# Post-norm decoder layer on one core: turned softmax blocks laid out in runs of 2 KB, two buffers for them

## The chip, the cores and the metric

The kernel runs on one core of one Trainium2 chip. The metric is the device time in microseconds (us) of one execution of the whole program; three runs were taken. All arrays are float32 unless said otherwise. The engines are named as in the profile: PE (matrix multiplications), DVE (vector), ACT (scalar), POOL (GpSimd), and SP, which here only issues DMAs; "SPq" and "ACTq" are the DMA issues of SP and ACT.

## What is computed

Eight slices `t` of 512 rows by 512 columns pass through three blocks, each followed by a residual sum and a layer norm. Cut to what matters:

```python
# 1: relative-position attention among the 8 slices, for each of the 512 positions
x = layernorm(x + attn(x, pos, ...))
# 2: cross-attention, for each t, to a context of 512 rows x 1024
k, v  = split((ctx @ W_src.T + b_src) * mask)          # 8 heads of 64
q     = (x @ W_tgt.T + b_tgt) * mask
p     = softmax(where(mask == 0, -inf, q k / 8))        # [8 heads, 512 queries, 512 keys]
upd   = p @ v                                           # [512, 512]
x = layernorm(x + concat([x, upd]) @ W_out.T + b_out)
# 3: feed-forward
h = float8(relu(x @ w1.T + b1))                         # 2048 wide
x = layernorm(x + float16(h @ float8(w2).T + float16(b2)))
```

The change is in block 2. There `p` comes out of the scores with the queries on the partitions, and the product `p @ v` needs it with the keys on the partitions, so every 128x128 piece of `p` has to be transposed.

## The kernel before

**Two stages.** Stage A (up to about 930 us) does block 1 and, interleaved, the keys and values of block 2 for t = 0 to 6, which go to DRAM (`kd`, `vd`). Stage B (from L630) does blocks 2 and 3 for all t and is where the change lies.

**A unit of attention.** Stage B cuts block 2 into 64 units `u = (t, c, jj)`: `c` is one of four pairs of heads, `jj` one half of the queries (two tiles `j = 2 jj, 2 jj + 1` of 128 queries). `scores` (L740) runs one unit:

- PE: four score products `s` into PSUM (L751).
- DVE: minimum of the negated scores, for each of the two tiles and two heads (`exponentials`, L763); ACT: the exponential, with its sum (L773), into a buffer `pe` of the pool `sp` (7 buffers).
- DVE: division by the sum (`divide`, L788), then `turn_blocks` (L800): a transposition of 32x32 blocks in place of partition, from `pe` into a tile `pb`. Four such instructions fill one `pb`. The pool `pb` has one buffer.
- SP: `move_blocks` (L805): after the block transposition, each 32x32 block is turned but stands in the wrong group of 32 partitions. 16 DMAs, SBUF to SBUF, each from 32 partitions `32 g` to 32 partitions `32 a`, put them into `pT`. Each moves 64 KB. `pT` has one buffer, which two units (jj = 0 and 1) fill half by half.

`attend` (L836) then multiplies `pT` with the values (`av`, L845, eight matmuls, 16 records in the trace) and ACT copies the result to `uT` (L852). So, for one (t, c): the moves of its first unit can begin once the `av` of the pair before has read `pT`, and `av` can begin once the moves of its second unit have landed.

**The order of work.** The order on PE, DVE, ACT and SP is written out by the kernel itself, one instruction stream per engine, in program order. `weave` (L1096) lays the units of attention of slice t between the "dense" steps: the output projection of slice t-1 (`project_out`, L857), the transposition of the next slice's rows (`turn`, L720), the query projections (`queries`, L726), and the feed-forward of slice t-1 (`hidden_steps`, L933) and t-2 (`finish`, L1012). The DVE parts of a unit are put into a list `side` and drawn from it bit by bit (`run`, L673); `settle` (L659) draws until no item of a name is left. A finished unit's moves go to a list `moves` and are issued at the next `run` for which `pT` is free (`move`, L669).

**What else SP issues.** SP works through its own list in order: the loads of keys and values (L716, L718), the weights of the feed-forward (L922, or L926 to L931 in the first round, which also wait for sums on POOL), the mask (L699), the stores of the result (L1045), and the rows of the next slice (`load_x1`, L712), which reuse the buffer from which the result of slice t-2 is stored. `next_x1` (L1088) draws the normalizations and stores of t-2 and then issues that load.

Of the kernel before, what the change touches and what calls it, by code (L numbers as in the profile page):

```python
# [9 lines left out]
F32 = mybir.dt.float32  # L10
# [7 lines left out]
P = 128  # L18
# [6 lines left out]
S, FS, H2, D2 = 512, 1024, 8, 64  # L25
# [17 lines left out]
def decoder_layer(  # L43
# [586 lines left out]
    with ExitStack() as ph:  # L630

        def pool(name, bufs, **kw):
            return ph.enter_context(
                tc.tile_pool(name=name, bufs=bufs, reuse_waits="tile", **kw)
            )
# [2 lines left out]
        qx = pool("qx", 1)  # L638
        mp = pool("mp", 1)
        kvd = pool("kvd", 2)  # L640
        sp = pool("sp", 7)
        pbp = pool("pb", 1)
        ptp = pool("ptp", 1)
        sm = pool("smb", 4)
        ps_mm = pool("b_mm", 2, space=PSUM)
# [13 lines left out]
        def settle(tag):  # L659

            for q in (urgent, side):
                while any(item[0] == tag for item in q):
                    q.pop(0)[2]()
# [46 lines left out]
        def load_x1(t):  # L710
            x1[t] = qx.tile([P, NJ, E], F32, tag="x1", bufs=3, name=f"x1{t}")
            nc.sync.dma_start(x1[t], x1d[t].rearrange("j p e -> p j e"))  # L712
# [27 lines left out]
        def scores(t, c, jj):  # L740
            if c == 0 and jj == 0:
                uT[t] = qx.tile([P, EC, S], F32, tag="uT", name=f"uT{t}")
            prs, pss = [], []
            u = (t * EC + c) * 2 + jj
            settle(("e", u - 1))
            js = [2 * jj, 2 * jj + 1]
            for j in js:

                ps = ps_s.tile([P, 2, S], F32, tag="s", name=f"s{t}_{c}_{j}")
                for h in range(2):  # L750
                    nc.tensor.matmul(  # L751
                        ps[:, h, :],
                        lhsT=qT[t][half[h], c, j * P : (j + 1) * P],
                        rhs=kT[t, c][half[h], :],
                        start=True,
                        stop=True,
                    )
                pss.append(ps)

            def exponentials(i, h):  # L760
                j, ps, (nmax, den, _) = js[i], pss[i], small[i]
                pe = sp.tile([P, S], F32, tag="pe", name=f"pe{t}_{c}_{j}_{h}")
                nc.vector.tensor_tensor_reduce(  # L763
                    out=pe,
                    in0=ps[:, h, :],
                    in1=mb[t],
                    scale=1.0,
                    scalar=FMAX,
                    op0=ALU.add,
                    op1=ALU.min,  # L770
                    accum_out=nmax[:, h : h + 1],
                )
                nc.scalar.activation(  # L773
                    pe,
                    pe,
                    AF.Exp,
                    bias=nmax[:, h : h + 1],
                    scale=-1.0,
                    accum_out=den[:, h : h + 1],
                )  # L780
                prs.append(pe)

            def divide(i):
                _, den, rden = small[i]
                nc.vector.reciprocal(rden, den)
                for h in range(2):
                    pe = prs[2 * i + h]
                    nc.vector.tensor_scalar(  # L788
                        pe, pe, rden[:, h : h + 1], None, ALU.mult
                    )  # L790

            def turn_blocks(i):


                if i == 0:
                    prs.append(
                        pbp.tile([P, 2, ST, 4, 2, 32], F32, tag="pb", name=f"pb{u}")
                    )
                for h in range(2):
                    nc.vector.transpose(  # L800
                        prs[4][:, h, :, :, i, :].rearrange("p k a e -> p (k a) e"),
                        prs[2 * i + h].rearrange("p (c e) -> p c e", e=32),
                    )

            def move_blocks():  # L805

                if jj == 0:
                    pT[t, c] = ptp.tile([P, 2, ST, S], F32, tag="pT", name=f"pT{t}_{c}")
                for a in range(4):
                    for g in range(4):  # L810
                        q0 = g * P + jj * 64
                        nc.sync.dma_start(  # L812
                            pT[t, c][32 * a : 32 * a + 32, :, :, q0 : q0 + 64],
                            prs[4][32 * g : 32 * g + 32, :, :, a].rearrange(
                                "p h k j e -> p h k (j e)"
                            ),
                        )


            small = [  # L820
                [
                    sm.tile([P, 2], F32, tag=n, name=f"{n}{t}_{c}_{j}")
                    for n in ("nmax", "den", "rden")
                ]
                for j in js
            ]
            for i, h in ((0, 0), (0, 1), (1, 0)):
                side.append((("e", u), 1.0, lambda i=i, h=h: exponentials(i, h)))
            side.append((u, 1.2, lambda: divide(0)))
            side.append((("e", u), 1.0, lambda: exponentials(1, 1)))  # L830
            side.append((u, 1.2, lambda: turn_blocks(0)))
            side.append((u, 1.2, lambda: divide(1)))
            side.append((u, 1.2, lambda: turn_blocks(1)))
            side.append((u, 0.0, lambda: moves.append((u, move_blocks))))

        def attend(t, c):  # L836

            nonlocal attended
            settle((t * EC + c) * 2 + 1)
            move()  # L840
            attended += 1
            av = mm(f"av{t}_{c}")
            for s in range(ST):
                for h in range(2):
                    nc.tensor.matmul(  # L845
                        av[half[h], :],
                        lhsT=v[t, c][:, s, half[h]],
                        rhs=pT[t, c][:, h, s, :],
                        start=(s == 0),
                        stop=(s == ST - 1),  # L850
                    )
            nc.scalar.copy(  # L852
                uT[t][:, c, :].rearrange("p (j g e) -> p g j e", j=NJ, g=4),
                av.rearrange("p (g j e) -> p g j e", g=4, j=NJ),
            )
# [229 lines left out]
                nc.sync.dma_start(b2f, rows[R_B2].partition_broadcast(P))  # L1085
                side.append((("b2", 0), 0.5, lambda: nc.vector.tensor_copy(b2q, b2f)))

        def next_x1(t):  # L1088

            settle(("y", t - 2))  # L1090
            load_x1(t + 1)

        def of(cost, f, *a):
            return [(cost, False, lambda: f(*a))]

# [50 lines left out]
        with tc.manual_schedule(engines={ET.PE, ET.DVE, ET.Activation, ET.SP}):  # L1146
# [11 lines left out]
            for t in range(T):  # L1158
# [51 lines left out]
                else:  # L1210
# [12 lines left out]
                    if early:  # L1223
                        dense += done[early - 1]
                    dense += out4[0]
                    if 1 < t < T - 1:
                        dense += of(0.0, next_x1, t)
                    dense += out4[1] + out4[2] + turns[0] + turns[1] + out4[3]
                    projected = len(dense)
                    dense += turns[2] + turns[3] + asked[0]  # L1230
                    rest = asked[1:-1] if t + 1 < T else done[early:]
# [140 lines left out]
```

## Time and profile before

| | |
|---|---|
| median of three runs | 2444.47 us (2444.20 to 2444.59) |
| the profiled execution | 2444.88 us |
| its span, first to last instruction | 2443.1 us |
| stage A, 0 to 930 us | PE busy 880.45 us |
| t = 0, window 930 to 1090 us | PE busy 118.22 of 160 us |
| t = 1, window 1190 to 1352 us | PE busy 122.87 of 162 us |
| t = 7, window 2150 to 2330 us | PE busy 134.74 of 180 us |
| tail, 2330 to 2443 us | PE busy 103.58 us |
| all DMA queues | q1 (issued by SP) 263.33 MB, 42.4% of the 16 DMA engines' time |

A line of a group reads: source line, engine, operation, output <- inputs, shapes, number of instructions, then after the bar the busy time of all, the mean of one in ns, and the idle time of the engine just before them with what ended most of it. A line of a timeline reads: start in us, length in us, engine, line, operation, number of instructions merged, and in brackets the idle time of the engine before it and what ended it. A line of SP's timeline merges neighbouring issues of one line, waits between them included.

### The profile page before, as it was taken

The numbers are of one execution on the slowest core, as the hardware profiler recorded it, in microseconds if no ns is written. First come the engines' busy times: TensorE is split into PE (matmuls) and PEld (weight loads), VectorE is DVE, ScalarE is ACT, GpSimd is POOL, SyncE is SP. The second block draws the span as 40 slices with busy tenths as digits, with TensorE's granted clock in tenths as the row PEclk, the third lists the DMA queues.
The fourth block names the chain that finished last, engine by engine and source line by source line (L and its number), as shares of the span: only waits on it lengthen the run. The fifth ranks groups of instructions, "written<-read, shape, count | busy, mean of one in ns | idle before, by whom it ended". The sixth has DMA issues, their size and how long they took to land.

```text
span 2443.1 us, 22426 instructions
## 1 busy us (share of the span) xinstructions
PE 2129.4 (87%) x7552; PEld 1218.5 (50%) x7552; DVE 1520.0 (62%) x2542; ACT 591.8 (24%) x1325; POOL 167.6 (7%) x156
## 2 busy tenths in 40 slices
PE   8999999999899998765868889889889898996698
PEld 5654764664575673222434354453544544533456
DVE  4899999999999933343435545546555464554324
ACT  2011111101111112121322342342433333413212
POOL 1001100110010000021020001001000000000000
PEclk9999999999999999887988999999999999998899
DMA  8031630341242376545454565464554655744512
GB/s 300 31 108 35 215 125 18 128 170 43 95 164 95 117 256 198 108 87 112 93 138 110 108 162 112 99 156 101 118 132 89 164 118 103 161 73 108 119 40 94
DMA packets 395204, 293.38 MB, mean 120 GB/s; under 512 B 288977, under 2 KB 317649, under 8 KB 395089
## 3 DMA queue, kind: packets, MB, share of 16 engines
q1 hardware_dynamic: 378864, 263.33, 42.4%
q10 hardware_dynamic: 16224, 28.61, 3.2%
q8 instruction: 60, 0.98, 0.2%
q14 instruction: 56, 0.45, 0.1%
HBM read 165.49 MB, written 59.24 MB: 92 GB/s over the span
## 4 chain that ended last, share of the span: by engine, by line
PE 49%; DVE 21%; SPq 13%; DMA 11%; issue 3%; ACT 2%; POOL 0%; DVEq 0%; ACTq 0%; POOLq 0%
SPq L812 13%; PE hx L942 6%; PE px L539 6%; PE av L845 6%; PE pz L539 3%; DMA pT<-pb 3%; DVE pv L428 3%; DVE pb L800 3%; PE ps_q L338 3%; PE hz L942 3%; PE psq L729 3%; PE po L454 2%; PE s L751 2%; DVE pv L438 2%; PE pox L865 2%
## 5 line engine op out<-in xcount | busy, mean ns | idle before, releaser
L800 DVE STREAM_TRANSPOSE pb<-pe 128x512 f32<-128x512 f32 x256 | 166.2, 687 | 258.7 <-DMA pT<-pb 254.5
L845 PE MATMUL av<-pT,vx 128*64 128x512 f32 x512 | 158.1, 774 | 169.8 <-DMA pT<-pb 169.8
L773 ACT ACTIVATE pe<-pe,nmax 128x512 f32<-128x512 f32 x256 | 183.2, 716 | 262.4 <-DVE nmax L763 256.4
L763 DVE CUSTOM_DVE_ANT_0 pe<-s,mb 128x512 f32<-128x512 f32 x256 | 167.7, 682 | 46.2 <-PE s L751 45.3
L942 PE MATMUL hx<-ffn 128*128 128x256 f32 x512 | 142.8, 402 | 45.1 <-DVE tm L996 25.2
L845 PEld LDWEIGHTS av<-pT,vx 128*64 128x64 f32 x512 | 47.2, 176 | 268.6 <-issue 236.6
L428 DVE TENSOR_TENSOR pv<-v,sc 128x2048 f32<-128x2048 f32 x64 | 148.5, 2320 | 2.0
L379 DVE TENSOR_TENSOR pq<-qw,k 128x2048 f32<-128x2048 f32 x64 | 146.4, 2288 | 1.1
L388 DVE TENSOR_REDUCE sc<-pq 128x64 f32<-128x2048 f32 x64 | 146.0, 2282 | 1.4
L942 PE MATMUL hx<-x2T,ffn 128*128 128x256 f32 x512 | 139.7, 396 | 4.1 <-ACT ffn L983 4.1
L942 PEld LDWEIGHTS hx<-ffn 128*128 128x128 f32 x512 | 92.2, 193 | 95.5 <-DVE tm L996 42.3
L751 PE MATMUL s<-kT,qTx 64*128 64x512 f32 x512 | 129.5, 621 | 8.3 <-DVE nmax L763 8.3
L788 DVE TENSOR_SCALAR pe<-pe,rden 128x512 f32<-128x512 f32 x256 | 118.7, 506 | 4.5
L1020 PE MATMUL o<-w2q,hq 128*128 128x512 fp8e4 x480 | 112.0, 392 | 8.3 <-DVE o L1030 8.3
L454 PE MATMUL po<-w_o,aoT 128*128 128x512 f32 x256 | 117.9, 603 | 0.8 <-ACT aoT L451 0.8
L729 PE MATMUL psq<-x1Ts,w_tgt 128*128 128x512 f32 x256 | 114.5, 597 | 4.7 <-ACT x1Ts L724 4.7
L338 PE MATMUL ps_q<-w_in,xt 128*128 128x512 f32 x256 | 116.7, 593 | 0.0
L865 PE MATMUL pox<-w_xo,x1Ts 128*128 128x512 f32 x256 | 116.0, 596 | 0.0
L942 PEld LDWEIGHTS hx<-x2T,ffn 128*128 128x128 f32 x512 | 91.5, 192 | 47.7 <-issue 14.1
L852 ACT COPY uT<-av 128x512 f32<-128x512 f32 x32 | 18.8, 587 | 397.9 <-PE av L845 397.9
L869 PE MATMUL pox<-w_xo,uT 128*128 128x512 f32 x256 | 115.1, 592 | 0.0
L338 PE MATMUL ps_k<-w_in,xt 128*128 128x512 f32 x256 | 114.0, 593 | 0.1
(180 smaller groups left out, 3235.1 us busy)
## 6 DMA issues: line engine op xcount, KB each, us to landing
pT<-pb SPq DMA_DIRECT2D x1024, 64.0 KB, 2.1
ffn<-w1d SPq DMA_DIRECT2D x56, 896.0 KB, 4.9
ch<-in_ctxT_dram SPq DMA_DIRECT2D x56, 256.0 KB, 3.3
td<-tx SPq DMA_DIRECT2D x28, 384.0 KB, 3.3
tx<-td SPq DMA_DIRECT2D x28, 384.0 KB, 5.2
r<-in_x_dram SPq DMA_DIRECT2D x32, 256.0 KB, 3.6
xt<-in_xT_dram SPq DMA_DIRECT2D x32, 256.0 KB, 2.7
x1d<-r ACTq DMA_DIRECT2D x32, 256.0 KB, 3.5
```

The costliest lines, as they stand in the source:

```text
L338: nc.tensor.matmul(ps, lhsT=xt[:, e, :], rhs=w_in[:, e, part * E : (part + 1) * E], start=(e == 0), stop=(e == EC - 1),)
L428: nc.vector.tensor_tensor(pr, v_all[:, :, fs].rearrange("p s (h d) -> p s h d", d=D1), sc[:, t, g * HH * T : (g + 1) * HH * T] .rearrange( ...
L454: nc.tensor.matmul(po, lhsT=aoT[:, c * P : (c + 1) * P], rhs=w_o[:, c, :], start=(c == 0), stop=(c == EC - 1),)
L539: nc.tensor.matmul(bank[:, first], lhsT=w7[:, a, f, ps] if part == 0 else b[f][:, ps], rhs=b[f] if part == 0 else w7[:, a, f, :], start=st ...
L729: nc.tensor.matmul(ps, lhsT=w_tgt[:, e, o * P : (o + 1) * P], rhs=x1T[t][:, e, :], start=(e == 0), stop=(e == EC - 1),)
L751: nc.tensor.matmul(ps[:, h, :], lhsT=qT[t][half[h], c, j * P : (j + 1) * P], rhs=kT[t, c][half[h], :], start=True, stop=True,)
L763: nc.vector.tensor_tensor_reduce(out=pe, in0=ps[:, h, :], in1=mb[t], scale=1.0, scalar=FMAX, op0=ALU.add, op1=ALU.min, accum_out=nmax[:, h ...
L773: nc.scalar.activation(pe, pe, AF.Exp, bias=nmax[:, h : h + 1], scale=-1.0, accum_out=den[:, h : h + 1],)
L800: nc.vector.transpose(prs[4][:, h, :, :, i, :].rearrange("p k a e -> p (k a) e"), prs[2 * i + h].rearrange("p (c e) -> p c e", e=32),)
L812: nc.sync.dma_start(pT[t, c][32 * a : 32 * a + 32, :, :, q0 : q0 + 64], prs[4][32 * g : 32 * g + 32, :, :, a].rearrange("p h k j e -> p h ...
L845: nc.tensor.matmul(av[half[h], :], lhsT=v[t, c][:, s, half[h]], rhs=pT[t, c][:, h, s, :], start=(s == 0), stop=(s == ST - 1),)
L942: nc.tensor.matmul(ps[:, 0:W], lhsT=ring[:, (t * HH2 + n) % RING, a, e, :], rhs=b[:, e, :], start=start and e == 0, stop=e == 1, skip_grou ...
```

## The change

Three edits and one that follows from them.

1. The tile `pb` has the target group `a` of partitions ahead, then the chunk of keys, the head, the tile and the 32 queries; `pT` has the source group `g`, the half `jj`, the chunk of keys, the head and 64 queries. What one DMA moves is then 2 KB in one run, on each of 32 partitions, on both sides; before it was eight runs of 256 bytes. The transposition writes, and `av` reads, through a pattern with strides: the right operand of `av` is eight pieces of 64 floats, 2 KB apart, where it was 512 floats in a row.
2. The pool `pb` has two buffers in place of one, the pool `sp` nine in place of seven.
3. The room for this, 12 KB per partition, comes from a scratch area for DMAs that GpSimd would issue, which is set to 1024 bytes; the kernel issues none from GpSimd.
4. `next_x1` is gone. Its `settle` stands where it stood, after the first output projection, but now for every t from 1 on; `load_x1` follows after the second output projection. In the built program the order on every engine stays the same but for one place on SP: in t = 2 to 6 the load L712 comes after the next unit's 16 moves, where it stood ahead of them.

```diff
-        sp = pool("sp", 7)
-        pbp = pool("pb", 1)
+        sp = pool("sp", 9)
+        pbp = pool("pb", 2)
...
-                        pbp.tile([P, 2, ST, 4, 2, 32], F32, tag="pb", name=f"pb{u}")
+                        pbp.tile([P, 4, ST, 2, 2, 32], F32, tag="pb", name=f"pb{u}")
                     )
                 for h in range(2):
                     nc.vector.transpose(
-                        prs[4][:, h, :, :, i, :].rearrange("p k a e -> p (k a) e"),
-                        prs[2 * i + h].rearrange("p (c e) -> p c e", e=32),
+                        prs[4][:, :, :, h, i, :].rearrange("p a k e -> p k a e"),
+                        prs[2 * i + h].rearrange("p (k a e) -> p k a e", a=4, e=32),
                     )
...
-                    pT[t, c] = ptp.tile([P, 2, ST, S], F32, tag="pT", name=f"pT{t}_{c}")
+                    pT[t, c] = ptp.tile(
+                        [P, 4, 2, ST, 2, 64], F32, tag="pT", name=f"pT{t}_{c}"
+                    )
                 for a in range(4):
                     for g in range(4):
-                        q0 = g * P + jj * 64
                         nc.sync.dma_start(
-                            pT[t, c][32 * a : 32 * a + 32, :, :, q0 : q0 + 64],
-                            prs[4][32 * g : 32 * g + 32, :, :, a].rearrange(
-                                "p h k j e -> p h k (j e)"
+                            pT[t, c][32 * a : 32 * a + 32, g, jj],
+                            prs[4][32 * g : 32 * g + 32, a].rearrange(
+                                "p k h j e -> p k h (j e)"
                             ),
                         )
...
-                        rhs=pT[t, c][:, h, s, :],
+                        rhs=pT[t, c][:, :, :, s, h].rearrange("p g i q -> p (g i) q"),
...
-        def next_x1(t):
-            settle(("y", t - 2))
-            load_x1(t + 1)
...
                     dense += out4[0]
+                    dense += of(0.0, settle, ("y", t - 2)) + out4[1]
                     if 1 < t < T - 1:
-                        dense += of(0.0, next_x1, t)
-                    dense += out4[1] + out4[2] + turns[0] + turns[1] + out4[3]
+                        dense += of(0.0, load_x1, t + 1)
+                    dense += out4[2] + turns[0] + turns[1] + out4[3]
...
-    nc = bacc.Bacc("TRN2", target_bir_lowering=False, num_devices=1)
+    nc = bacc.Bacc(
+        "TRN2", target_bir_lowering=False, num_devices=1,
+        dynamic_dma_scratch_size=1024,
+    )
```

## The prediction

> **What bounds the kernel now.** I read the page's busy times and chain first, then its groups, then the times of SP's issues, then the timelines of PE, DVE and SP over one slice.
>
> ```profile
> PE 2129.4 (87%) x7552; PEld 1218.5 (50%) x7552; DVE 1520.0 (62%) x2542; ACT 591.8 (24%) x1325; POOL 167.6 (7%) x156
> ...
> PE 49%; DVE 21%; SPq 13%; DMA 11%; issue 3%; ACT 2%; POOL 0%; DVEq 0%; ACTq 0%; POOLq 0%
> ...
> L800 DVE STREAM_TRANSPOSE pb<-pe 128x512 f32<-128x512 f32 x256 | 166.2, 687 | 258.7 <-DMA pT<-pb 254.5
> L845 PE MATMUL av<-pT,vx 128*64 128x512 f32 x512 | 158.1, 774 | 169.8 <-DMA pT<-pb 169.8
> ```
>
> PE is the bound, with 13% of the chain in SP's issues, nearly all of them the moves of L812. Two waits belong to the moves: PE stands 169.8 us ahead of `av` (32.0 more are booked on its weight loads), and DVE 254.5 us ahead of the transposition, because the single `pb` is still being read. The second costs only where it hides something PE needs.
>
> ```profile
> L812 SPq DMA_DIRECT2D pT<-pb x1024: 585/609/1878, 947.2 to 2324.5; - x171
> ...
> L1045 SPq DMA_DIRECT2D out_dram<-x x32: 332/360/672, 1343.8 to 2440.0; - x32
> ```
>
> These are the least, median and largest time of one issue on SP, in ns. A move holds SP for 0.609 us and 0.045 more pass before the next: a pitch of 0.655, so 16 moves take 10.4 us. A plain store with 2 KB per partition holds it 0.33 to 0.36 us. Now PE, DVE and SP in the slice t = 3:
>
> ```profile
> 1528.98 3.65 PE L845 MATMUL av<-pT,vx 128*64 128x512 f32 x16
> 1569.76 6.37 PE L845 MATMUL av<-pT,vx 128*64 128x512 f32 x16 [7.68 <-DMA pT<-pb]
> 1608.28 5.35 PE L845 MATMUL av<-pT,vx 128*64 128x512 f32 x16 [2.48 <-DMA pT<-pb]
> 1650.57 5.18 PE L1020 MATMUL o<-w2q,hq 128*128 128x512 fp8e4 x16 [2.66 <-DVE o L1030]
> ...
> 1556.30 1.29 DVE L800 STREAM_TRANSPOSE pb<-pe 128x512 f32<-128x512 f32 x2
> 1648.64 1.30 DVE L800 STREAM_TRANSPOSE pb<-pe 128x512 f32<-128x512 f32 x2 [6.61 <-DMA pT<-pb]
> ...
> 1533.48 34.52 SPq L812 DMA_DIRECT2D pT<-pb  x32
> 1635.62 11.22 SPq L812 DMA_DIRECT2D pT<-pb  x16
> ```
>
> The reader should see three stalls per slice. (1) `av` of c = 1: the last transposition ends at 1557.5, the 16 moves follow, the last is issued at 1567.4, lands 2.1 later, and PE starts at 1569.8. (2) The same for c = 2, 2.48 us. (3) `o` waits 2.66 us for DVE, which itself stood 6.61 us for `pb`. Each stall also lengthens what follows: 16 records of `av` take 3.65 us when PE came without a pause, 5.3 to 6.6 after pauses over 2 us (3.65 again after 1.8 and 2.29).
>
> **What the Trainium skill says.** "DMA: Bandwidth & Descriptors", Anatomy of one DMA, gives a fixed cost of about 2 us per DMA, mostly the write's receipt; the median landing of 2.1 us agrees, and I leave that part as it is. The same page, Why a DMA increments its semaphore by 16, says that a DMA is spread over the largest number of engines up to 16 that divides its slowest dimension; that is 32 partitions before and after, so all 16 serve it both times; the DMA share of 0.65 in 1533.5 to 1543.5 us, where only moves ran (115 GB/s), fits. "SBUF — State Buffer", Door 1, says 32 partitions reach 8 of 16 ports, measured at 189 GB/s: 64 KB in 0.347 us, my floor for the pitch; no run here shows it. "TensorE: Matmul & The Clock Gate", What's actually happening, says that an idle PE falls to half clock and needs about 3.4 us of work to recover: the longer `av` above agrees.
>
> **The change part by part.**
>
> *Issue of a move.* 1024 issues go from eight runs of 256 bytes to one run of 2 KB on each partition. No row shows such a move. Bounds: nothing gained (pitch 0.655), and the shortest DMA issue in the trace, 0.319 us (the stores to `td`) plus 0.045. I take 0.37, since plain rows of 2 KB cost 0.33. From the first issue to the last landing that is 15 x (0.655 - 0.37) = 4.3 us less; where SP's list itself is late, 16 x 0.285 = 4.6. Every DMA also waits for the eighth DMA ahead of it on its queue (the program's order of waits shows it): 8 x 0.37 = 3.0 us against 2.1 to land, so this doesn't bind, except behind a large load (a weight load lands in 4.9 us), where I add 1 to 3 us.
>
> *Second `pb`.* It takes away DVE's waits. It counts only where PE waits for DVE next.
>
> *Strided operands.* `bd` (L369) reads its operand in pieces of 8 floats and takes 273 ns for 128 columns; the contiguous transpositions of 128 columns take 280 to 285. So `av` at nothing. The 256 transpositions write pieces of 128 bytes with strides before and after: nothing; DVE's idle time covers up to 0.3 us each. Bounds for both together: 0 to 15 us.
>
> *`sp` at nine buffers, the smaller scratch:* nothing; `pe` shows only 1.0 us of buffer-like waiting on ACT.
>
> *Load of the next rows (five times).* It moves behind 16 moves. Before, in t = 3: stores until 1679.9, load issued at 1682.2 once they had landed, PE waits 1.19 us at 1688.7. After, DVE is not held by `pb`, so the second transposition ends near 1674.4, the stores are issued by 1676.9, the moves by 1682.9 and the load at 1683.0: 0.8 later. Cost 0.8 each (-1 to 3), 4 us in all. The kT and vx loads behind it wait for `av` anyway.
>
> Now place by place, in us. Where a stall is removed I count what it adds to the following 16 records too.
>
> - t = 0. Stalls of 11.40, 9.46, 12.85, 30.93 before the four `av`. c = 0: DVE waited 4.8 for `pb`; without it the second transposition ends near 967 in place of 971.5, landing 975 against PE ready at 974.2: gain 12. c = 1: moves start 3.4 sooner and take 4.3 less, PE no longer waits: 12.3. c = 2: last transposition at 1050.2 (was 1054.8), `av` at 1058.3: 8.5. c = 3: SP's list is late; unit 6's moves save 4.6, then 17.7 us of weight loads and POOL's sums stay, and unit 7's moves stand behind a 1 MB load, where the eighth-DMA wait takes part of the gain back: 7.5. Sum 40.3.
> - t = 1. 1.2 for c = 0. c = 1 as stall (1): 4.3 + 0.7 of clock = 5.0. Then a stall of 8.03 on hx (DVE held by `pb`) and 13.08 at c = 2; behind both stands SP's list, two moves around 17 us of weight loads: 2 x 4.6 less 1.2 = 8.0. Then 5.53 on hx, again `pb`, and 2.8 of cold records: 8.3. Sum 22.5.
> - t = 2 to 5. Stall (1): 5.0 each, and about 3.4 of idle PE stays. Stall (2): 2.29, 2.48, 2.57, 2.06 all gone with 1.7 of clock three times: 14.5. Stall (3): 2.01, 2.66, 1.65, 2.03 and 3.2 of clock: 11.6. One hx stall of 1.77. Sum 47.9.
> - t = 6. 5.0, then 2.24 + 1.7, then 4.16 + 2.4 at c = 3: 15.5.
> - t = 7. c = 1 (12.98): bound by DVE's last transposition at 2220.3, so one move, 4.3. c = 2 (13.80): transposition about 2 sooner plus 4.3: 6.2. Then hx 3.96, cold records and 1.81 at c = 3: 7.4. Sum 17.9.
>
> Total 144.1, less 4 for the load of rows: 140. On the profiled execution (2444.88, 1.8 around its span) that gives 2304.9; the median stands 0.4 below it, which I neglect. Forecast 2305. What is late next is PE itself: in t = 2 to 5 about 155 us per slice, with the rest of stall (1), the waits of 0.52 on `tm` and the 1.2 for the rows.
>
> **The rivals.**
>
> *The issue stays at 0.655.* For it: issue times don't follow the number of runs strictly (vx, 512 runs of 512 bytes, 577 ns; a masked broadcast row 543). Against: plain DMAs of 2 KB rows show medians of 0.33 to 0.38 (one, kT, 0.44). Only the second `pb` pays: t = 0 about 12, t = 1 8.3, stall (3) and hx 13.4, t = 7 7.6, some 42: 2403.
>
> *The transfers become the limit.* Issued faster, the moves share 8 ports for reading and writing, land later, and the eighth-DMA wait holds SP; with a pitch of 0.50, fifteen bound moves lose 15 x 0.13 = 1.95 each, 29 us: 2334. For it: only the floor of 0.347; against: DMA share 0.65 with eight times the packets.
>
> *Slower: `av` reads its pieces slowly.* Its place is L845, 32 times on PE's path. The gain of 140 is eaten when `av` takes 140/32 = 4.4 us longer, from 3.6 to 8. At three times the length, +230, the kernel would take 2535. Against it stands the row of `bd`; for it, only that no trace shows pieces of 256 bytes 2 KB apart.
>
> **How the numbers follow.** Forecast 0.77, unchanged issue 0.08, transfer limit 0.10, slow `av` 0.05 (0.04 of it slower than before). The forecast's own ends: pitch 0.48 costs 23, half of the 27 us of clock effects 14, so 2342; pitch 0.33 with the load of rows free gives about 2290, and a little more if DVE running ahead frees other stalls. The range is 2272 to 2350; it takes in the transfer limit and leaves the other two out. What this kernel's measurement can tell from no change is about 0.2%, 5 us: faster 0.95, same 0.01, slower 0.04.
>
> **What would show it.** L812 near 0.33 us per issue; no wait of L800 for pT<-pb; `av` without a pause at c = 2 and with 3 to 4 us at c = 1; `o` not waiting for L1030; L845 at 3.6 us per 16 records when PE came warm; L800 still near 690 ns; `xtr` waiting 1 to 2 us for the rows. The forecast fails if the issue stays above 0.5 us, or if SP shows waits inside a group of 16 moves.

## The result, and the profile after

| | before | after |
|---|---|---|
| median of four runs each | 2444.53 us (2444.20 to 2444.91) | 2420.43 us (2415.46 to 2425.11) |
| the profiled execution | 2444.88 us | 2425.11 us |
| its span | 2443.1 us | 2423.3 us |

The ratio is 0.9901, with a 95% interval of 0.9875 to 0.9927: 24 us faster, where 140 were forecast. The forecast of 2305 us and its range (to 2350) both missed. The single runs of the kernel after lie 10 us apart, those of the kernel before 0.7 us in this comparison, but 17 us in a later one; so differences under some 5 us are not read below.

The lines of after that answer to those of before. First the issues of a move (least, median and largest time of one on SP, in ns); then, from the page, the engines of the chain and the groups:

```profile
L813 SPq DMA_DIRECT2D pT<-pb x1024: 507/589/1662, 951.0 to 2301.7; - x171
```

```profile
PE 55%; DVE 19%; SPq 11%; DMA 10%; issue 3%; ACT 2%; POOL 0%; DVEq 0%; ACTq 0%; POOLq 0%
...
L845 PE MATMUL av<-pT,vx 128*64 128x512 f32 x512 | 153.1, 753 | 148.5 <-DMA pT<-pb 148.5
...
L800 DVE STREAM_TRANSPOSE pb<-pe 128x512 f32<-128x512 f32 x256 | 166.1, 687 | 1.5 <-issue 1.5
```

The issue decides the case. It takes 589 ns, where 609 were before and 325 were assumed (a pitch of 0.37 less 0.045). The prediction itself named an issue above 0.5 us as the sign of its failure. DVE's wait for `pb` is gone (254.5 us before). But PE still stands 148.5 us ahead of `av` (169.8 before). The packets fell from 395204 to 165827 and the share of SP's queue from 42.4% to 36.1%: the transfers did become cheaper, but the issues did not.

Now slice t = 3, PE first, then SP, with the start, the length and the wait ahead of it in brackets:

```profile
1509.47 3.65 PE L845 MATMUL av<-pT,vx 128*64 128x512 f32 x16
1549.76 6.36 PE L845 MATMUL av<-pT,vx 128*64 128x512 f32 x16 [7.18 <-DMA pT<-pb]
1587.80 3.65 PE L845 MATMUL av<-pT,vx 128*64 128x512 f32 x16 [2.00 <-DMA pT<-pb]
...
1667.03 1.97 PE L723 MATMUL xtr<-ident,x 128*128 128x128 f32 x8 [6.07 <-DMA x<-x1d]
...
1648.64 2.44 SPq L1045 DMA_DIRECT2D out_dram<-x  x4
1651.13 10.02 SPq L813 DMA_DIRECT2D pT<-pb  x16
1661.19 0.58 SPq L712 DMA_DIRECT2D x<-x1d  x1
```

Stall (1) is 7.18 us, where it was 7.68, and stall (2) 2.00, where it was 2.48. A group of 16 moves takes 10.02 us, where it took 10.39. Stall (3) is gone from `o`. A new one has come: `xtr` waits 6.07 us for the rows of the next slice. SP has the four stores out at 1651.1, then works 10 us at moves, and only then issues the load.

Where `av` starts, kernel after ahead of kernel before, in us (start in before less start in after):

| t | 0 | 1 | 2 | 3 | 4 | 5 | 6 | 7 |
|---|---|---|---|---|---|---|---|---|
| c = 0 | 1.8 | 18.3 | 19.5 | 19.5 | 19.6 | 17.6 | 14.1 | 16.7 |
| c = 3 | 17.4 | 28.4 | 26.3 | 26.6 | 24.0 | 21.6 | 16.0 | 22.9 |

The lead grows to 28.4 us by the end of t = 1. Then each slice from t = 2 to 6 wins 2 to 7 us between its c = 0 and its c = 3, and each of the five steps over a load of rows (from c = 3 of t = 1 to c = 0 of t = 2, and so on up to t = 6) takes 6.4 to 8.9 back. At the end of the program it is 19.8.

### The profile page after: what moved, and what is told of

It reads as the page before. It is cut to its first block, busy times and chain, and to the rows that moved or that the text cites. A ratio compares the mean times of both kernels' runs of the same rounds, so it can differ in the third digit from the quotient of the medians.

```text
span 2423.3 us, 22413 instructions
## 1 busy us (share of the span) xinstructions
PE 2130.3 (88%) x7552; PEld 1220.6 (50%) x7552; DVE 1518.1 (63%) x2542; ACT 592.2 (24%) x1325; POOL 167.9 (7%) x156
## 2 busy tenths in 40 slices
DMA packets 165827, 293.38 MB, mean 121 GB/s; under 512 B 26832, under 2 KB 55504, under 8 KB 165712
## 3 DMA queue, kind: packets, MB, share of 16 engines
q1 hardware_dynamic: 149488, 263.33, 36.1%
## 4 chain that ended last, share of the span: by engine, by line
PE 55%; DVE 19%; SPq 11%; DMA 10%; issue 3%; ACT 2%; POOL 0%; DVEq 0%; ACTq 0%; POOLq 0%
SPq L813 10%; PE hx L942 7%; PE av L845 6%; PE px L539 6%; PE pox L865 3%; DVE pv L428 3%; PE hz L942 3%; PE pox L869 3%; PE pz L539 3%; PE o L1020 3%; PE s L751 3%; PE ps_q L338 3%; PE psq L729 3%; PE po L454 2%; DMA pT<-pb 2%
## 5 line engine op out<-in xcount | busy, mean ns | idle before, releaser
L845 PE MATMUL av<-pT,vx 128*64 128x512 f32 x512 | 153.1, 753 | 148.5 <-DMA pT<-pb 148.5
L428 DVE TENSOR_TENSOR pv<-v,sc 128x2048 f32<-128x2048 f32 x64 | 148.5, 2320 | 2.0
L865 PE MATMUL pox<-w_xo,x1Ts 128*128 128x512 f32 x256 | 123.3, 626 | 0.0
L979 DVE TENSOR_TENSOR ffn<-hx,ffn 128x256 f32<-128x256 f32 x64 | 27.2, 424 | 150.8 <-PE hx L942 128.7
L338 PE MATMUL ps_v<-w_in,xt 128*128 128x512 f32 x256 | 111.6, 594 | 0.0
```

The lines of the kernel that those rows point to most:

```text
L338: nc.tensor.matmul(ps, lhsT=xt[:, e, :], rhs=w_in[:, e, part * E : (part + 1) * E], start=(e == 0), stop=(e == EC - 1),)
L428: nc.vector.tensor_tensor(pr, v_all[:, :, fs].rearrange("p s (h d) -> p s h d", d=D1), sc[:, t, g * HH * T : (g + 1) * HH * T] .rearrange( ...
L845: nc.tensor.matmul(av[half[h], :], lhsT=v[t, c][:, s, half[h]], rhs=pT[t, c][:, :, :, s, h].rearrange("p g i q -> p (g i) q"), start=(s == 0),
L865: nc.tensor.matmul(po, lhsT=x1T[t][:, e, js], rhs=w_xo[:, e, :], start=(e == 0), stop=False)
```

## The experiments

The theory: a DMA between partitions of SBUF occupies SP for about 0.6 us whatever the length of its runs. So the layout shortens next to nothing on SP, and the load of rows behind 16 moves comes 10 us late. The rivals are told with each run. A comparison is always with the kernel before on the same chip (median of 2440.2 to 2443.0 us there), as a ratio.

**1. The order of the load taken back** (`e1_rows_first`). `next_x1` comes back as it was before.

```diff
-                    dense += of(0.0, settle, ("y", t - 2)) + out4[1]
-                    if 1 < t < T - 1:
-                        dense += of(0.0, load_x1, t + 1)
-                    dense += out4[2] + turns[0] + turns[1] + out4[3]
+                    if 1 < t < T - 1:
+                        dense += of(0.0, next_x1, t)
+                    dense += out4[1] + out4[2] + turns[0] + turns[1] + out4[3]
```

> The changed kernel with the load of the next rows (x1) put back ahead of the unit's 16 moves, as it was before; layout and two pb buffers stay. Theory: a move's issue costs 0.59 us whatever its runs are, so a load queued behind 16 moves comes 9 to 10 us later; in the trace of the changed kernel PE waits 5.6 to 6.1 us for it in five slices (0.5 to 1.4 before) and restarts cold, some 6.5 us per slice lost. Expected: 30 us faster than the changed kernel, about 2390 (0.978 of before), the wait for x<-x1d back under 2 us. Rival (the loss in those slices is due to something else, such as PE's order or DVE): the same as the changed kernel within 8 us.

Measured: 2378.82 us, ratio 0.973 (0.9706 to 0.9755). The fourth edit therefore costs 42 us, 8.4 in each of five slices, more than expected. In the trace of this kernel the load goes out between the stores and the moves, and PE comes to `xtr` without a pause:

```profile
1631.56 2.07 SPq L1045 DMA_DIRECT2D out_dram<-x  x4
1635.79 0.38 SPq L712 DMA_DIRECT2D x<-x1d  x1
1636.21 11.75 SPq L813 DMA_DIRECT2D pT<-pb  x16
...
1643.72 1.04 PE L723 MATMUL xtr<-ident,x 128*128 128x128 f32 x8
```

From the first store to the load it is 4.2 us here and 12.6 after: 8.3 us. What a slice loses by that is PE's wait for the rows (28.6 us in the five slices of after, none here) and the slower records behind such a pause: the eight `xtr` took 1.97 us after it and take 1.04 here.

**2. Two buffers alone** (`e2_two_pb_alone`): the kernel before with edits 2 and 3.

```diff
-        sp = pool("sp", 7)
-        pbp = pool("pb", 1)
+        sp = pool("sp", 9)
+        pbp = pool("pb", 2)
...
+        dynamic_dma_scratch_size=1024,
```

> The kernel before with two pb and nine pe buffers only (layout of 256-byte runs, order of the load of rows as before). Theory: the whole gain of the change is that DVE no longer waits for pb; expected about 2400 (0.982), faster than the changed kernel because the load of rows stays ahead. Rival (the longer runs carry part of the gain): 2430 or more.

Measured: 2410.31 us, ratio 0.9859 (0.9835 to 0.9883), so 32 us, 10 short of what was expected. That this is the whole gain, as the expectation has it, doesn't hold: experiment 3 shows another.

**3. The layout alone** (`e3_layout_alone`): edit 1 and nothing else.

```diff
-                        pbp.tile([P, 2, ST, 4, 2, 32], F32, tag="pb", name=f"pb{u}")
+                        pbp.tile([P, 4, ST, 2, 2, 32], F32, tag="pb", name=f"pb{u}")
...
-                    pT[t, c] = ptp.tile([P, 2, ST, S], F32, tag="pT", name=f"pT{t}_{c}")
+                    pT[t, c] = ptp.tile(
+                        [P, 4, 2, ST, 2, 64], F32, tag="pT", name=f"pT{t}_{c}"
+                    )
...
```

> The kernel before with the layout of 2 KB runs only (one pb, seven pe, load of rows ahead as before). Theory: the issue falls by 0.02 us per move only, 15 x 0.02 = 0.3 us at each of some 20 places, so 2436 to 2442 (0.997 to 0.999). Rival (the layout is worth more, the change lost it elsewhere): under 2425. Rival (strided operands cost): over 2450.

Measured: 2410.78 us, ratio 0.9869 (0.9846 to 0.9891), so 31 us. This expectation missed: the layout is worth more than the 0.02 us per issue. Experiments 1 to 3 add up: 32 + 31 = 63, and experiment 1, which has both, is 63 us faster than before. Between the two traces, whose spans differ by 35 us, 14 arise by the end of t = 0 (`av` of c = 3 starts at 1112.98 in place of 1126.86), and some 3 in each later slice. Experiment 8 asks where from.

**4. The price of an issue by itself** (`p1_issue_probe`): a program of DMAs alone.

```python
dst[q(n), n], src[q(n + 1), n % 4]              # L40: 32 partitions, one run of 2 KB
dst[q(n), n] as 8 x 256 B, src as 8 x 256 B     # L43
dst[q(n), n, 0:64], src[q(n + 1), n % 4, 0:64]  # L49: one run of 256 B
dst[:, n], src[:, n % 4]                        # L56: 128 partitions, 2 KB
dst[q(n), n], dd[n, q(n + 1)]                   # L62: from DRAM, 32 partitions, 2 KB
dd[n, q(n + 1)], src[q(n), n % 4]               # L68: to DRAM, 32 partitions, 2 KB
```

> Only DMAs, eight of a shape in a row, everything of the layer is left out; the output is a copy of parts of x. What sets the 0.59 us of an issue. Theory A (source and destination both in SBUF): all SBUF-to-SBUF shapes cost 0.55 to 0.65 us, with 32, 64 or 128 partitions, and 32 partitions to or from DRAM cost 0.33 to 0.40. Theory B (fewer than 128 partitions): 32 partitions cost 0.55 to 0.65 to and from DRAM too, and 128 partitions within SBUF cost 0.33 to 0.40. Theory C (the size or number of runs): 32 partitions with a single run of 256 bytes cost clearly less than 0.5.

Measured, least, median and largest time of one issue in ns:

```profile
L40 SPq DMA_DIRECT2D dst<-src x16: 533/585/589, 8.6 to 96.9; - x16
L43 SPq DMA_DIRECT2D dst<-src x16: 608/609/672, 16.9 to 105.4; - x16
L49 SPq DMA_DIRECT2D dst<-src x16: 560/588/590, 25.1 to 113.4; - x16
L56 SPq DMA_DIRECT2D dst<-src x16: 478/604/616, 41.1 to 129.4; - x16
L62 SPq DMA_DIRECT2D dst<-dd x16: 323/419/423, 56.5 to 143.5; - x16
L68 SPq DMA_DIRECT2D dd<-src x16: 302/421/437, 65.8 to 156.5; - x16
```

Between L40 and L43 only the length of the pieces differs: 24 ns, about the step from 609 to 589 that the kernel shows. L49 moves an eighth of the bytes and L56 four times as many: 588 and 604. L62 and L68 have the partitions and the rows of L40, with DRAM on one side: 420, a little over the 0.33 to 0.40 that was expected. With 128 partitions those with DRAM have 430 (load) and 498 (store). So the side makes the difference, not the runs; and even with DRAM an issue in a row costs more than the 0.33 of the forecast. Those of the same form on ACT's queue had a median of 602. The Trainium skill, "Perfetto Trace Analysis", DMA Instruction — HWDGE, says that the profiled issue covers the making of the descriptors and not the movement of the data; that the bytes leave the issue alone agrees. Why an SBUF-to-SBUF pair is dearer, neither it nor a run here says.

**5. Fewer issues** (`e4_pool_diagonal`, `e7_pool_six`, `e8_pool_eight`, `e10_pool_ten`): these stand on the kernel of experiment 1. Some of a unit's 16 blocks are copied by POOL, which is busy for 7% of the span in after; SP issues the rest.

```diff
+                        if a == g:
+                            nc.gpsimd.tensor_copy(dst, blk)
+                        else:
+                            nc.sync.dma_start(dst, blk)
```

Six take two more pairs (a, g), eight those with `(a - g) % 4 < 2`, ten also (2, 0) and (0, 2).

> The kernel after with the load of rows ahead of the moves again, as in e1_rows_first, and of each unit's 16 moves the four that stay on their own 32 partitions (a == g) are copies on POOL, which has little to do in this stage; SP issues 12. Theory A (the number of SBUF-to-SBUF issues on SP sets the time of a move, about 0.63 us each, whatever their layout): a group takes 12 x 0.63 = 7.6 us in place of 10.1, 2.5 us off every stall that waits for a group, at some 15 to 24 places: 2320 to 2345, with L813's median still 0.58 to 0.60. Rival B (what remains of the stalls is set by the landing of the last move or by DVE, not by SP's issues; or POOL's copies, four of 0.7 to 1.7 us each by POOL's rows, take the moves' place): 2370 or more.

> As e4_pool_diagonal, with two more moves of each unit as POOL copies (from partitions 0 to 31 into 32 to 63, and 64 to 95 into 96 to 127); SP issues 10. Theory A: a group takes 10 x 0.63 = 6.3 us; if POOL's six copies take no longer than that, 5 to 20 us less than e4; if POOL's copies are over 1.1 us each they end after SP's moves and it is no faster than e4. Rival B: as for e4, 2370 or more.

> As e7_pool_six, with eight of the 16 moves of a unit as copies on POOL and eight left to SP. Theory A (a stall ends when SP's last move lands: issues x 0.63 us and 2 us to land, against POOL's 0.616 us per copy): SP's group takes 8 x 0.63 = 5.1 us, landed at 7.1, POOL ends at about 5; 1.2 us less than with six at some 12 to 15 places: 2270 to 2280. Rival B (DVE's last transposition sets what is left, or POOL's copies end last): 2285 or more.

> As e8_pool_eight, with ten copies on POOL and six moves on SP. Theory A: SP's group takes 3.8 us and has landed at 5.8, POOL's ten copies end at 6.2, so av can start 0.9 us sooner than with eight: 2260 to 2275. Rival B (POOL starts later than SP, or a copy's end reaches PE later than 0.2 us): the same as e8 or slower.

| moves on SP | 16 (experiment 1) | 12 | 10 | 8 | 6 |
|---|---|---|---|---|---|
| us | 2378.82 | 2312.17 | 2291.03 | 2267.58 | 2265.64 |
| ratio to before | 0.973 | 0.9459 | 0.9372 | 0.9294 | 0.9278 |
| 95% interval | 0.9706 to 0.9755 | 0.9439 to 0.9479 | 0.9351 to 0.9394 | 0.9272 to 0.9315 | 0.9251 to 0.9306 |
| PE ahead of `av`, us | 151.5 | 99.2 | 80.8 | 63.4 | 66.7 |

The layout and the order stay, only the number of SP's issues falls, and the time follows it down to eight, for twelve, ten and eight somewhat beyond what was expected. Fewer moves also change whose turn of semaphores falls where (experiment 8), but SP's waits on stores in t = 0 were only 4.0 us with 16 moves, and 0.5 to 0.7 with twelve to eight. The page of the kernel with eight:

```profile
L818 POOL COPY pT<-pb 32x512 f32<-32x512 f32 x512 | 317.2, 620 | 693.9 <-DVE pb L800 420.7
...
L847 PE MATMUL av<-pT,vx 128*64 128x512 f32 x512 | 127.0, 641 | 63.4 <-DMA pT<-pb 62.9
```

and SP and POOL at one unit of it:

```profile
1492.44 5.16 SPq L820 DMA_DIRECT2D pT<-pb  x8
...
1492.47 5.15 POOL L818 COPY pT<-pb 32x512 f32<-32x512 f32 x8 [14.52 <-DVE pb L800]
```

A copy takes 620 ns, as much as an issue, so the two work side by side and a unit's moves are issued in half the time. Of PE's waits ahead of `av` 62.9 us on moves remain. With ten on POOL the trace puts 23.1 of PE's 66.7 us on copies (0.5 at most with eight), so that POOL now ends last in places, and no gain over eight can be told. The kernels with eight and ten are faster than before and after: 7% below before.

**6. The load of rows behind eight moves** (`e9_eight_rows_behind`): the kernel with eight copies, with the fourth edit.

> The kernel after, with its fourth edit kept (the load of rows behind the next unit's moves), and eight of 16 moves as copies on POOL; beside e8_pool_eight it has that one place on SP changed. Theory A (what the fourth edit costs is the time that SP needs for the moves ahead of the load): with 16 moves of 10.1 us it cost 42 us in five slices, 8.4 each, so about 1.7 of the 10.1 were hidden; with 8 moves of 5.1 us it costs 3.4 each, 17 us in all: e8 plus 12 to 25. Rival B (the cost is not the moves ahead of it, but that the stores of slice t-2 or the load itself come later for another reason): e8 plus 35 to 45.

Measured: 2278.53 us, ratio 0.934 (0.9316 to 0.9364), 11 us above its neighbour; with 16 moves it was 42. That is a little under the 12 to 25 of theory A and far from its rival. `xtr` now waits 6.9 us in all, where it was 28.6. The edit's price is set by the issues that it puts ahead of the load; it fell faster than their number, from 8.4 us in a slice to 2.2:

```profile
1572.15 2.58 SPq L1047 DMA_DIRECT2D out_dram<-x  x4
1574.78 4.95 SPq L820 DMA_DIRECT2D pT<-pb  x8
1579.78 0.58 SPq L712 DMA_DIRECT2D x<-x1d  x1
```

**7. Do the transfers matter?** (`e5_thin_moves`) The kernel of experiment 1 with moves of an eighth of the bytes; the rest of the blocks is left out of the product.

```diff
-                            pT[t, c][32 * a : 32 * a + 32, g, jj],
-                            prs[4][32 * g : 32 * g + 32, a].rearrange(
+                            pT[t, c][32 * a : 32 * a + 32, g, jj, 0:1, 0:1],
+                            prs[4][32 * g : 32 * g + 32, a, 0:1, 0:1].rearrange(
...
-                        rhs=pT[t, c][:, :, :, s, h].rearrange("p g i q -> p (g i) q"),
+                        rhs=pT[t, c][:, :, :, 0, 0].rearrange("p g i q -> p (g i) q"),
```

> e1_rows_first with moves that carry 256 bytes of the 2 KB on each partition (one chunk of keys and one head), still 16 per unit; av reads that piece for all chunks and heads, so the rest of the transposed blocks is left out of the product and PE's work is the same. Theory A (issue count): L813's median stays 0.58 to 0.60 and the time within 15 us of e1's 2379, 2364 to 2379; what it gains is landing time and room on the DMA engines beside loads. Rival B (the 64 KB of a move and the DMA engines' time matter): L813 below 0.5 us or a time under 2350.

Measured: 2345.72 us, ratio 0.9602 (0.9581 to 0.9622). This one is split. The issue stays, as theory A has it:

```profile
L813 SPq DMA_DIRECT2D pT<-pb x1024: 507/589/1687, 946.9 to 2229.7; - x171
```

but the time falls 33 us below experiment 1, more than the 15 it allowed and just into the rival's. That is not the bytes alone, for the edit did a second thing: a thin move reads only what the first head's transpositions wrote, so it doesn't wait for the last one. The second unit of c = 1 in t = 3, first in experiment 1, then here:

```profile
1519.05 1.29 DVE L800 STREAM_TRANSPOSE pb<-pe 128x512 f32<-128x512 f32 x2
1520.37 10.00 SPq L813 DMA_DIRECT2D pT<-pb  x16
1532.03 5.31 PE L845 MATMUL av<-pT,vx 128*64 128x512 f32 x16 [7.19 <-DMA pT<-pb]
...
1505.62 1.29 DVE L800 STREAM_TRANSPOSE pb<-pe 128x512 f32<-128x512 f32 x2
1506.34 10.00 SPq L813 DMA_DIRECT2D pT<-pb  x16
1517.72 5.87 PE L845 MATMUL av<-pT,vx 128*64 128x512 f32 x16 [6.32 <-DMA pT<-pb]
```

In experiment 1 the moves start 0.03 us after the pair of transpositions, here 0.57 before its end; so it is in 27 of the 64 units. Of the 0.87 us that PE waits less, 0.6 are this earlier start and the rest is the landing, 1.8 us in place of 2.0. An estimate by these shares gives the bytes some 10 of the 33 us, within the 15 of theory A; the run doesn't separate the two.

**8. What the layout gains in t = 0.** The first guess was that 256-byte pieces get little room beside large transfers. `e6_before_small_w2` cuts the four loads of w2 in the kernel before to a quarter each, and `p2_contention_probe` measures 16 moves of either layout alone, beside a store and beside a load.

```diff
-            nc.sync.dma_start(w2f[q], chunked(w2T)[:, q * 4 : q * 4 + 4, :])
+            nc.sync.dma_start(w2f[q][:, 0:1], chunked(w2T)[:, q * 4 : q * 4 + 1, :])
```

> The kernel before with a quarter of each of the four 1 MB loads of w2 in t = 0 (the rest of w2 is left out and a quarter is used four times by the conversion). It asks why the layout alone gave about 14 us in t = 0. Theory A (256-byte packets get little of the DMA engines beside a large load, so moves land late there and SP waits inside a group): the groups of 16 moves that took 13.3 and 13.4 us in before take 10.4 to 11 here, and the av of c = 3 in t = 0 starts 4 to 8 us sooner than in before. Rival B (the loads have nothing to do with it): the groups still take over 13.

> Only DMAs; of the layer nothing is computed, and the time says nothing. Six blocks, each twice, of 16 moves of 64 KB between partitions on SP, with 2 KB in one run or in eight runs of 256 bytes on each partition: alone, with one 256 KB store to DRAM on ACT's queue at their start, and with one 1 MB load on SP ahead of them. Theory A (256-byte pieces get little of the DMA engines beside larger transfers, so moves land late and SP waits inside the group): alone both take 10 to 10.4 us; beside the store 10 against 12 to 14; beside the load 10 to 14 against 2 to 5 us more. Rival B (the run length doesn't matter beside other traffic): the two layouts within 0.7 us of each other in all three pairs.

Both speak against it. In the first, two groups fall, from 17.93 to 14.88 and from 12.05 to 10.40 us, but the two of 13.3 and 13.4 us still take 13.15 and 12.64, and the ratio to before is 0.9976 (0.9962 to 0.999), 6 us. In the probe (L54 and L57 alone, L64 and L68 beside the store) the layouts differ by 0.4 to 0.8 us:

```profile
10.71 10.06 SPq L54 DMA_DIRECT2D dst<-src  x16
24.02 10.49 SPq L57 DMA_DIRECT2D dst<-src  x16
37.47 10.06 SPq L64 DMA_DIRECT2D dst<-src  x16
50.78 10.86 SPq L68 DMA_DIRECT2D dst<-src  x16
```

beside the load by 0.3 at most. The trace of before, asked for SP's own waits in t = 0 (total, times, longest), names something else:

```profile
SPq L812 <- DMA kd<-kst: 9.3, 3, 5.4
SPq L812 <- DMA vd<-vst: 8.8, 4, 3.6
```

and in a group that took 13.29 us SP stops once. These are the eleventh and the twelfth move, and the store that ACT issues between them:

```profile
999.58 0.61 SPq L812 DMA_DIRECT2D pT<-pb  x1
1003.02 1.37 SPq L812 DMA_DIRECT2D pT<-pb  x2
...
1000.04 0.33 ACTq L169 DMA_DIRECT2D kd<-kst  x1
```

The waits in the built program give the reason. The DMAs of SP and ACT take eight semaphores in turn, in the order of the program, and each waits until the DMA that had its semaphore before has landed. The twelfth move and this store share one:

```
SP:  335 L812 DMACopy pT0_1_4547<-pb2_4513 32x8x64 [waits DMAHW4_49]
ACT: 400 L169 DMACopy kd7_94<-kst7_3_4544 128x512 [waits DMAHW4_49,Activation_49]
```

ACT issues the store when PE's product is there, so the move waits for PE and then for 256 KB to land. In the new layout alone the turns fall otherwise: this store has semaphore 0, and the next to want it is the load of w2 behind the group, over 3 us after the store's issue. Two kernels issue the eight stores of t = 7 from POOL, which takes them out of these turns, in the old and in the new layout; a third does so in the kernel with eight copies.

```diff
-            nc.scalar.dma_start(kd[t][:, o, :], st)
+            (nc.gpsimd if t == 7 else nc.scalar).dma_start(kd[t][:, o, :], st)
```

> The kernel before with the eight stores of the keys and values of t = 7 (L169, L183, on ACT's queue) issued from POOL, whose DMAs have semaphores of their own. Theory A (SP's moves and ACT's stores take eight semaphores in turn, so a move waits for the landing of a store that ACT issues late; the layout changed only whose turn falls where): SP no longer waits for kd or vd stores inside a group (18.1 us in before), the groups that took 13.3 and 13.4 us take 10.4 to 11, and the time is 8 to 14 us less than before's, 2427 to 2434. Rival B (256-byte pieces land late beside the stores' traffic): the groups still take 13 us and the time is within 3 us of before's.

> The same change to e3_layout_alone (the new layout and nothing else). Theory A: its waits on stores were few (3.6 us), so it gains 0 to 5 us on e3, 2405 to 2411, and the layout is worth 17 to 25 us between e11 and e12 in place of 31. Rival B: the layout is still worth 28 us or more between e11 and e12.

> The same change to e8_pool_eight. Theory A: little is left to gain, 0 to 5 us less than e8's 2267.6. Rival B (POOL works in order, so its copies of blocks stand behind stores that wait for PE and ACT): 2270 or more.

Measured: old layout 2433.03 us, 0.9962 (0.9946 to 0.9977), 10 us less than before; new layout 2406.53, 0.9853 (0.9834 to 0.9872), by the medians 4 less than experiment 3, which the intervals don't tell from nothing. The waits on stores are gone from SP's list in both, and the two groups of the old layout take 11.4 and 10.4:

```profile
986.49 11.38 SPq L812 DMA_DIRECT2D pT<-pb  x16
...
1003.28 10.43 SPq L812 DMA_DIRECT2D pT<-pb  x16
```

Between the two the layout is worth 26.5 us in place of 31: outside both expectations (17 to 25, or 28 and more). So the turn of semaphores is shown as a part: it costs the old layout 10 us and the new one 4 or nothing, so it is some 6 to 10 of the 31, a difference not far above the noise. The rest can be placed in the traces, though no run separates its pieces. Where a group starts right behind the last transposition, it is 0.37 us shorter (10.02 for 10.39) and a move lands about 0.1 us sooner (2.0 for 2.1); PE's wait at c = 1 of t = 2 to 6 is 0.3 to 0.5 us shorter. Of the 26 us between these two kernels, 20 are idle time of PE (256.3 us from 930 us on in the old layout, 236.3 in the new), 12 of them ahead of `av` (158.2 to 146.5). Most of what is left is PE's busy time, with a mean granted clock of 0.953 in place of 0.949: at c = 2 of t = 2, 5 and 6, for one, the pause was 2.06 to 2.25 us and is 1.60 to 1.82, and the 16 records of `av` behind it take 3.65 us in place of 5.35. The third kernel, 2266.23 us (0.9281, 0.926 to 0.93), can't be told from its neighbour.

## Why the prediction was wrong

*Issue of a move* is the step that failed: "I take 0.37, since plain rows of 2 KB cost 0.33." The pitch measured is 0.633 (a group takes 10.02 us), so 15 x 0.022 = 0.3 us are saved on the issues in place of 4.3. The rows that it was taken from were stores and loads with DRAM on one side; the nearest row to an SBUF-to-SBUF move was the move itself, and the bound "nothing gained" was the true one. Experiment 4 shows it, and experiment 5 shows that the rest of the step, what a shorter group is worth, was sound to some 20 us: a group of 5.9 us, the 16 x 0.37 of the forecast, lies between the kernels of experiment 5 with ten issues (6.3 us, 2291) and eight (5.1, 2268), at about 2283 by a straight line. The forecast without its row-load term was 2301.

*Load of the next rows* failed too, 0.8 us where 8.4 came, 4 in all where 42 came. It follows in part from the same number: 16 moves of 5.9 us were put ahead of the load, not of 10.0. The rest is the yardstick: I compared with the load in the kernel before, which goes out at 1682.2 because its stores come late. With DVE ahead, the stores came early, and an early load was there to be had; experiment 1 takes it. The delay should have been costed against a kernel that has the second `pb`, not against the kernel before.

*Second `pb`* was right in kind. DVE's wait went from 254.5 us to nothing, and stall (3) with it; alone it is worth 32 us, where 42 stood. One wait that I didn't count is in the trace of experiment 2: SP waits 30.0 us in t = 0 for the stores of `kd` and `vd` (16.4 + 13.6), 18.1 before. In this trace `av` of c = 3 in t = 0 starts 0.5 us ahead of the kernel before, where the prediction had some 12 for t = 0. So the missing 10 are in t = 0; that those waits are the reason is argued, not shown.

*The layout* as a whole was given 102 us (144.1 less 42) and brought 31, and not by a cheap issue: by 0.02 us per issue, 0.1 per landing, what follows from these on PE, and turns of semaphores that I hadn't counted. Without these 31 us the sum would be 32 less 42: that the kernel came out faster at all rests on a gain that the forecast had for another reason, and this much of it was luck.

*The wait for the eighth DMA ahead* was taken for one within SP's queue. Experiment 8 shows that ACT's DMAs take turns in the same eight semaphores; so SP waited 18.1 us for ACT's stores in t = 0 before, and the prediction has no term for it. The fixed 2 us per DMA were right, though the section of the Trainium skill that is cited for them ("DMA: Bandwidth & Descriptors", Anatomy of one DMA) describes DMAs that GpSimd issues: here the landing took 2.1 us before and 2.0 after.

*Strided operands* at nothing was right: the transposition takes 687 ns in both kernels, and 16 records of `av` 3.65 us when PE came warm. `sp` and the scratch were in experiment 2 together with the buffer and not tried apart.

*The rival "issue stays"* was the true course, with a chance of 0.08, and it too was priced wrongly: 2403, since it put the load of rows at nothing, though by its own number the load stood behind 10.5 us of moves, and since it gave the layout nothing. What was measured gives 2444.5 - 32 - 31 + 42 = 2423, near the 2420 found. The transfer limit didn't show (no group of 16 slowed by the faster issue, since there was none), nor slow `av`.

## What to carry to other kernels

Take the price of a DMA's issue from a DMA with the same two sides, and if the profile has none but the very move in question, count its present price as the likeliest: the layout of the runs changed it by 24 ns of 609. When a queue's issues are the limit, issue fewer of them: an idle engine that copies part of the blocks gave 111 us here where the layout gave 31. An edit that puts a load behind other issues of its queue delays it by their whole time, and costs what of that isn't covered (8.4 us of 10.0 here, 2.2 of 5.0 with eight moves); so it must be costed after the other edits, together with them. And when you thin a transfer to see what its bytes cost, look in the trace at what it now waits for: here it no longer waited for its last producer, and most of the gain came from that.

## What was unexpected of the hardware

- An issue between partitions takes 0.585 to 0.609 us whatever its bytes (8 to 256 KB), partitions (32 to 128) or runs (1 or 8), one with DRAM on a side 0.42 in a row with 32 partitions (0.43 and 0.50 with 128), and SP's queue and ACT's are alike (585 and 602 ns).
- POOL copies 32 partitions x 512 floats in 620 ns, into its own partitions (613) or another 32 (means of 616 to 621 in the mix), and DVE's transposition beside it keeps its 686 ns.
- Beside a 256 KB store or a 1 MB load, 16 moves in pieces of 256 bytes take at most 0.8 us longer than in pieces of 2 KB.
